# Four-layer graph network on one core: a group's last weighing placed in one TensorE block with the next group's first scores, and new plan constants

## The chip, the cores and the metric

The kernel runs on one core of one Trainium2 chip. The time is the device time of one execution in microseconds (us), the median of three runs. The engines are named as in the profile: PE is TensorE (matrix multiply), PEld its weight load, DVE is VectorE, ACT is ScalarE, POOL is GpSimd, SP is SyncE, which issues the transfers. PSUM is the memory into which PE writes, and which DVE and ACT read.

## The reference, cut to what matters

128 graphs of 64 nodes with 256 features pass four layers, each with its own layer norm, ReLU and residual. Everything is float32.

```python
def reference(x, adj, nodemask, ...):          # x (128, 64, 256), adj (128, 64, 64)
    h = relu(layernorm(x))
    # layer 0: attention, 8 heads of 32, with a mask
    q, k, v = (split_heads(h @ W + b) for W, b in ...)
    scores = einsum('bhqd,bhkd->bhqk', q, k) / sqrt(32)
    attn = softmax(where(adj > 0, scores, NEG))
    x = x + (attn @ v, heads merged) @ Wo + bo
    # layer 1: the same with log(adj + 1e-6) added to the scores
    # layer 2: five steps of a gated graph network
    h = relu(layernorm(x))
    for l in range(5):
        m = h @ weight[l]
        agg = einsum('bij,bid->bjd', adj != 0, m)
        h = gru_cell(agg, h, w_ih, w_hh, b_ih, b_hh)
    x = x + h * nodemask
    # layer 3: a gated graph convolution with three 256 x 256 products
    ...
    return x
```

"Scores" are the products q k, "weighing" is the product of the softmax with v.

## The kernel before

The 128 graphs are worked in 16 groups of 8 graphs (512 tokens). Each group has a front (layers 0 and 1), a chain of five gated steps (layer 2) and a back (layer 3). The kernel doesn't run these in program order: every operation is first recorded in a plan, with a key (where it stands in the pipeline, in units of one group's time), an estimated duration, and what it reads and writes. `Plan.run` then deals the operations out, engine by engine, so that the front of one group, the steps of another and the back of a third stand interleaved in each engine's instruction stream. The order is fixed when the program is built.

```python
INTO, OUT, BESIDE, ALONE = 110, 260, 0.3, 0.1    # ns for going into and out of small matmuls, and weights of choice
AHEAD = 1.5                                       # how far ahead of the oldest operation one may be taken
FRONT, FRONT_LAST, FRONT_SPAN = -0.1, -0.05, 1.0
BACK, BACK_LAST, BACK_SPAN = -0.1, 0.6, 0.5
STEP, STEP_LAST, STEP_SPAN = -0.2, -0.05, 0.4
LOCK, BACK_END, ENTRY = 0.35, 0.05, -0.15
FIRST, FIRST_SPAN = -1.0, 1.05
ORDER = (0, 0, 1, 0, 1, 0)                        # (assignments gathered in one place here)
...
    def bank(name):                               # PSUM: four banks for everything but the gates
        return new("a", [P, 512], 4, name)

    def gate(name):                               # and four for the gates of layer 2
        return new("g", [P, TOK], 4, name)
```

Most matmuls use the whole array (128 rows, 128 columns). Three kinds are small: the scores (64 x 64), the weighing (64 x 32) and the neighbour sum of layer 2, `agg` (64 x 64). The plan marks them `small=True`. Layer 0 or 1 for half a group is one call of `attend`:

```python
    waiting = []

    def attend(layer, xt, half, bias, bias_at, name):
        hT = normed(xt, half, name, True)         # layer norm, ReLU, transposed (lnT on PE)
        ...                                       # q and k products, evacuated to qT and k_exp
        pss = [bank(f"s_{name}_{i}") for i in range(2)]

        def scores():
            ...
                            nc.tensor.matmul(ps[gp * NODES : (gp + 1) * NODES, 2 * c : 2 * c + 2, i, :],   # L585
                                             qT[s, c, t0 : t0 + NODES], k_exp[s, c, :, t0 : t0 + NODES], ...)

        es = [new("e", [P, 4, 2 * NODES], 3, f"e_{name}_{i}") for i in range(2)]
        if waiting:
            weigh_last, reads, po_last, oT_last, finish_last = waiting.pop()

            def both():
                weigh_last()
                scores()

            pe(1440, both, [*reads, qT, k_exp], [*po_last, *pss], holds=[oT_last, *es], small=True)
            finish_last()
        else:
            pe(870, scores, [qT, k_exp], pss, holds=es, small=True)
        ...                                       # v product; softmax on DVE, ACT, POOL; aT: softmax transposed on PE
        po = [bank(f"o_{name}_{i}") for i in range(2)]

        def weigh():
            ...
                            nc.tensor.matmul(o[q * HD : (q + 1) * HD, c, s],                              # L659
                                             v[rows, gp, h * HD : (h + 1) * HD],
                                             aTs[q // 2][rows, 2 * c + q % 2, s], ...)

        def finish():
            ...                                   # oT: evacuated by DVE; y = oT Wo (L672); x = y + x (L675)

        waiting.append((weigh, [v, *aTs], po, oT, finish))

    def flush():
        weigh, reads, po, oT, finish = waiting.pop()
        pe(470, weigh, reads, po, holds=[oT], small=True)
        finish()
```

So the weighing of one half is kept back in `waiting` and placed in one block with the scores of the next half. `both` takes the banks of both, four in all. A group's four halves (two layers, two halves) are driven by `front`, which also loads x for the next group:

```python
    def front(g):
        ...
        for layer in range(2):
            ...
            for half in range(2):
                ...
                attend(layer, xt, half, bias, bias_at, f"{g}_{layer}_{half}")
                yield
        flush()
        if g + 1 < n_groups and g:
            load_x(g + 1)
        ...                                       # A, degrees, adjT (transposed adjacency) for layers 2 and 3
```

and the fronts are recorded one after another:

```python
    parts = {g: front(g) for g in range(n_groups)}
    with plan.strand(FIRST, FIRST_SPAN):
        for g in ORDER:                           # all of group 0, two halves of group 1
            next(parts[g])
        for _ in parts[0]:
            pass
    ...
    begin = {g: g - (LOCK if g + 1 == n_groups else 0.0) for g in range(n_groups)}
    events = sorted([(begin[g] + 0.4 * l, g, l) for g in range(n_groups) for l in range(LAYERS)] +
                    [(begin[g] - 1.001, g, -1) for g in range(1, n_groups)])
    for at, g, l in events:
        last = g + 1 == n_groups
        if l < 0:
            with plan.strand(begin[g] - 1 + FRONT + (FRONT_LAST if last else 0), FRONT_SPAN):
                for _ in parts[g]:
                    pass
            continue
        ...                                       # the entry to layer 2, its five steps, and the back
```

The back uses the four banks too. Its products for half a group, seven in place of eight, accumulate in two of them; DVE adds a saved part and writes F (L1059):

```python
        def total(bk, t, o, i):
            vec(dve(384), lambda: nc.vector.tensor_tensor(
                F[i][:, :, o * P : (o + 1) * P], part(bk), t[:, :3, :], op=ALU.add), [bk, t], [(F[i], o)])
        ...
        product(3, pc)                            # l3c on PE (L1047)
        total(pc, u, 0, 1)
```

Of the kernel before, what the change touches and what calls it, by code (L numbers as in the profile page):

```python
# [44 lines left out]


INTO, OUT, BESIDE, ALONE = 110, 260, 0.3, 0.1
AHEAD = 1.5

FRONT = -0.1
FRONT_LAST = -0.05
FRONT_SPAN = 1.0
BACK = -0.1
BACK_LAST = 0.6
BACK_SPAN = 0.5
STEP = -0.2
STEP_LAST = -0.05
STEP_SPAN = 0.4  # L60
LOCK = 0.35
BACK_END = 0.05
ENTRY = -0.15
FIRST = -1.0
FIRST_SPAN = 1.05
ORDER = (0, 0, 1, 0, 1, 0)
FUSE = -1.05
FUSE_SPAN = 0.45
# [53 lines left out]
class Plan:  # L122
# [62 lines left out]
    def run(self):  # L185
# [12 lines left out]
        for _ in range(len(self.ops)):  # L198
            while due[0] in done:
                due.pop(0)  # L200
            best, horizon = None, due[0].key + AHEAD
            for eng, ops in ready.items():
# [52 lines left out]
def gnn_stack_kernel(ctx: ExitStack, tc: tile.TileContext, a: dict, out: bass.AP):  # L255
# [3 lines left out]
    n_groups = n_pairs // PAIRS  # L259
# [14 lines left out]
    def new(tag, shape, n, name=None):  # L274
        if tag not in tags:
            home = psum if tag in ("a", "g") else dram if tag == "gates" else work
            tags[tag] = Slots(home, tag, n, tag in ("g", "ht", "agg", "Ta", "Th", "gv", "qT", "kexp", "v"))
        return Val(tags[tag], name or tag, shape)

    def bank(name):  # L280
        return new("a", [P, 512], 4, name)
# [4 lines left out]
    def pe(cost, fn, reads, writes, early=0.0, holds=(), small=False):  # L286
        plan.add("PE", cost, fn, reads, writes, early=early, holds=holds, small=small)
# [4 lines left out]
    def vec2(cost, fn, reads, writes, early=0.0):  # L292

        plan.add("DVE", cost, fn, reads, writes, early=early, port=True)
# [4 lines left out]
    def pool(cost, fn, reads, writes, early=0.0):  # L299
        plan.add("POOL", cost, fn, reads, writes, early=early, port=True)  # L300

    def dma(kb, fn, reads, writes, n=1):
        plan.add("SP", max(450 * n, 60 + kb * 5), fn, reads, writes)
# [6 lines left out]
    def load_adj(i):  # L310
        t = new("adjq", [P, n_adj, NODES], 2, f"adjq{i}")
        dma(256, lambda: nc.sync.dma_start(t.tile, adj_t[:, i * n_adj : (i + 1) * n_adj, :]), [], [t])
        adj_vals[i] = [t, None]
# [7 lines left out]
    def load_x(g):  # L321
        t = new("x", [P, PAIRS, D], X_BUFS, f"x{g}")
        x_vals[g] = t
        for half in range(2):
            p = slice(2 * half, 2 * half + 2)
            dma(256, lambda p=p: nc.sync.dma_start(
                t[:, p, :], x_t[:, g * PAIRS + p.start : g * PAIRS + p.stop, :]),
                [], [(t, p.start), (t, p.start + 1)])
# [201 lines left out]
    waiting = []  # L530

    def attend(layer, xt, half, bias, bias_at, name):
# [25 lines left out]
        v = new("v", [P, 2, D], 2, f"v_{name}")  # L558
# [18 lines left out]
        def scores():  # L577
            for i in range(2):
                for c in range(2):
                    for gp in range(2):  # L580
                        for rh in range(2):
                            s = slice(rh * 2 * HD, (rh + 1) * 2 * HD)
                            t0 = (2 * gp + i) * NODES
                            ps = pss[rh].tile.rearrange("p (h i k) -> p h i k", h=4, i=2)
                            nc.tensor.matmul(ps[gp * NODES : (gp + 1) * NODES, 2 * c : 2 * c + 2, i, :],  # L585
                                             qT[s, c, t0 : t0 + NODES], k_exp[s, c, :, t0 : t0 + NODES],
                                             start=True, stop=True)

        es = [new("e", [P, 4, 2 * NODES], 3, f"e_{name}_{i}") for i in range(2)]
        if waiting:  # L590
            weigh_last, reads, po_last, oT_last, finish_last = waiting.pop()

            def both():
                weigh_last()
# [6 lines that stand above are left out]
# [14 lines left out]
        aTs = []  # L615
# [33 lines left out]
        po = [bank(f"o_{name}_{i}") for i in range(2)]  # L649
# [13 lines left out]
        oT = new("oT", [P, 2, 2, P], 1, f"oT_{name}")  # L663
# [12 lines left out]
                xt[:, pp : pp + 2, :], py.tile.rearrange("p (t d) -> p t d", t=2), xt[:, pp : pp + 2, :],  # L676
                op=ALU.add), [py, (xt, pp), (xt, pp + 1)], [(xt, pp), (xt, pp + 1)])

        waiting.append((weigh, [v, *aTs], po, oT, finish))

    def flush():
        weigh, reads, po, oT, finish = waiting.pop()
        pe(470, weigh, reads, po, holds=[oT], small=True)
        finish()

# [261 lines left out]
    def front(g):  # L947

        if g % ADJ_GROUPS == 0 and (g // ADJ_GROUPS + 1) * ADJ_GROUPS < n_groups:
            load_adj(g // ADJ_GROUPS + 1)  # L950
        xt = x_vals.pop(g)
        adjq = adj_vals[g // ADJ_GROUPS][0]
        sel = slice((g % ADJ_GROUPS) * PAIRS, (g % ADJ_GROUPS + 1) * PAIRS)
        first = (g % ADJ_GROUPS) * PAIRS
        neg = new("neg", [P, PAIRS, NODES], 1, f"neg_{g}")
        vec2(200, lambda: nc.vector.tensor_scalar(
            neg.tile, adjq[:, sel, :], 0.0, NEG, op0=ALU.is_le, op1=ALU.mult), [adjq], [neg])
        for layer in range(2):
            if layer and not g % ADJ_GROUPS:
                log_adj(g // ADJ_GROUPS)  # L960
            ladj = adj_vals[g // ADJ_GROUPS][1]
            for half in range(2):
                bias = ladj if layer else neg
                bias_at = (lambda p, t=ladj, n=first: t.tile.rearrange("p t k -> p (t k)")[:, (n + p) * NODES : (n + p + 2) * NODES]) if layer else (
                    lambda p, t=neg: t.tile.rearrange("p t k -> p (t k)")[:, p * NODES : (p + 2) * NODES])
                attend(layer, xt, half, bias, bias_at, f"{g}_{layer}_{half}")
                yield
        flush()
        if g + 1 < n_groups and g:
            load_x(g + 1)  # L970
        for gp in range(2):
            s = slice(gp * NODES, (gp + 1) * NODES)
            pool(530, lambda s=s: nc.gpsimd.tensor_copy(blk[s, :, s], adjq[s, sel, :]), [adjq], [(blk, gp)])

        A = new("A", [P, PAIRS, NODES], 3, f"A_{g}")
        vec2(250, lambda: nc.vector.tensor_scalar(A.tile, adjq[:, sel, :], 0.0, None, op0=ALU.not_equal),
             [adjq], [A])
        deg = new("deg", [P, PAIRS], 2, f"deg_{g}")
        vec(310, lambda: nc.vector.tensor_reduce(
            deg.tile, adjq[:, sel, :], axis=AX.X, op=ALU.add, apply_absolute_value=True), [adjq], [deg])  # L980
        norm = new("norm", [P, PAIRS], 5, f"norm_{g}")
        power(norm, deg, lambda: deg.tile, 1e-6, PAIRS, f"deg_{g}")
        adjT = new("adjT", [P, PAIRS, P], 4, f"adjT_{g}")
        ps = bank(f"adjT_{g}")

        def turn():
            for p in range(PAIRS):
                nc.tensor.transpose(ps[:, p * P : (p + 1) * P], blk[:, p, :], ident.tile)

        pe(437, turn, [blk, ident], [ps], holds=[adjT])  # L990

        for p in range(PAIRS):
            sca(act(P, 1), lambda p=p: nc.scalar.activation(
                adjT[:, p, :], ps[:, p * P : (p + 1) * P], AF.Identity, scale=norm[:, p : p + 1]),
                [ps, norm], [(adjT, p)])
        held[g] = xt, A, adjT, norm
# [138 lines left out]
    parts = {g: front(g) for g in range(n_groups)}  # L1135
    with plan.strand(FIRST, FIRST_SPAN):
        for g in ORDER:
# [8 lines left out]
    with plan.strand(0.5, 0.1):  # L1146
        combine(w3, lambda b: w3[:, :, b, :], 7, made)

    begin = {g: g - (LOCK if g + 1 == n_groups else 0.0) for g in range(n_groups)}
    events = sorted([(begin[g] + 0.4 * l, g, l) for g in range(n_groups) for l in range(LAYERS)] +  # L1150
                    [(begin[g] - 1.001, g, -1) for g in range(1, n_groups)])
    for at, g, l in events:
        last = g + 1 == n_groups
        if l < 0:
            with plan.strand(begin[g] - 1 + FRONT + (FRONT_LAST if last else 0), FRONT_SPAN):
                for _ in parts[g]:
                    pass
            continue
        if l == 0:
            xt, A, adjT, norm = held[g]  # L1160
            with plan.strand(begin[g] + ENTRY, 0.1):
                h, ht = entry(g, xt)
            held[g] = xt, h, adjT, norm
            chains[g] = gru(h, ht, A, str(g))
        with plan.strand(at + STEP + (STEP_LAST if last else 0), STEP_SPAN):
            next(chains[g])
        if l + 1 == LAYERS:
            with plan.strand(begin[g] + 2 + BACK + (BACK_LAST if g + 2 == n_groups else BACK_END if last else 0), BACK_SPAN):
                back(g, *held.pop(g))
# [34 lines left out]
```

## Time and profile before

| | |
|---|---|
| median of 3 runs | 2578.69 us (2578.02 to 2578.84) |
| span of the profiled execution | 2576.9 us |
| PE busy | 2540.9 us |
| PEld busy | 2135.8 us |
| DVE busy | 1866.1 us |
| ACT busy | 1315.1 us |
| POOL busy | 837.8 us |
| mean granted TensorE clock | 0.996 |
| HBM traffic over the span | 55 GB/s |

Busy time is the time in which an engine has at least one instruction in work. Matmuls are pipelined, and each record lasts longer than its share of the stream, so what a matmul costs is read from start to start in the timeline, not from its length. Each matmul of the program leaves two records in the trace. In the timeline a row is a run of like instructions: its start, its length, engine, line, operation, what is written and read, the shapes, the number of records, and in brackets the idle time before it and what ended that.

### The profile page before, as it was taken

Reading aid. Unit: us, or ns where it says so; the run is one execution under the profiler, and the core shown is the slowest. Engines: PE = TensorE matmul, PEld = TensorE weight load, DVE = VectorE, ACT = ScalarE, POOL = GpSimd, SP = SyncE. Lnnn points to the kernel's source line nnn. Section 1 sums busy time; section 2 is a strip of 40 time slices with the busy share of each in tenths; the row PEclk is TensorE's granted clock in tenths of the full one; section 3 lists DMA queues with packets and bytes.
Section 4 is the critical chain, followed back from the end, with each engine's and each line's share of the span. In section 5 each row is a group of like instructions: output and inputs, shape, how many; then the busy total and the mean of one; then the engine's idle time right before and its main releaser. Section 6 shows DMA issues by size and latency. Waiting matters only on the chain.

```text
span 2576.9 us, 54509 instructions
## 1 busy us (share of the span) xinstructions
PE 2540.9 (99%) x22445; PEld 2135.8 (83%) x22445; DVE 1866.1 (72%) x4137; ACT 1315.1 (51%) x2452; POOL 837.8 (33%) x890
## 2 busy tenths in 40 slices
PE   8999999999999999999999999999999999999997
PEld 6788888888888888888888888888888888888885
DVE  5676678777776876778677776777768767776766
ACT  4455454554545546555554545545455455555543
POOL 5442333323232332432323333332323323223220
PEclk9999999999999999999999999999999999999998
DMA  5221211111111111112111111111111111111110
GB/s 155 104 78 44 70 48 57 44 48 60 48 56 44 61 48 48 56 44 68 63 47 57 48 56 48 48 56 48 56 44 60 44 48 56 44 48 70 55 62 17
DMA packets 44203, 145.54 MB, mean 56 GB/s; under 512 B 11106, under 2 KB 32820, under 8 KB 33076
## 3 DMA queue, kind: packets, MB, share of 16 engines
q1 hardware_dynamic: 43840, 142.03, 15.7%
q8 instruction: 177, 2.90, 0.5%
q14 instruction: 70, 0.57, 0.1%
q10 hardware_dynamic: 116, 0.04, 0.0%
HBM read 126.79 MB, written 15.27 MB: 55 GB/s over the span
## 4 chain that ended last, share of the span: by engine, by line
PE 95%; DVE 2%; ACT 2%; issue 0%; DMA 0%; POOL 0%; SPq 0%; DVEq 0%; ACTq 0%; POOLq 0%
PE gb L782 21%; PE gc L782 16%; PE nb L782 10%; PE nc L782 8%; PE q L544 4%; PE k L544 4%; PE y L672 4%; PE v L605 4%; PE agg L822 3%; PE l3b L1047 3%; PE s L585 3%; PE hT L488 2%; PE l3c L1047 2%; PE aT L640 2%; PE lnT L488 2%; PE o L659 2%
## 5 line engine op out<-in xcount | busy, mean ns | idle before, releaser
L891 POOL TENSOR_TENSOR sn<-h,sn 128x512 f32<-128x512 f32 x160 | 205.7, 1286 | 666.8 <-ACT sn L889 666.5
L634 POOL TENSOR_TENSOR e<-e,ssum 128x512 f32<-128x512 f32 x128 | 142.9, 1127 | 344.4 <-DVE ssum L633 279.5
L782 PE MATMUL gb<-Th,w_hh 128*128 128x256 f32 x960 | 247.5, 380 | 1.4 <-DVE sg L854 1.4
L782 PE MATMUL gb<-Ta,gv 128*128 128x256 f32 x960 | 248.0, 381 | 0.0
L751 POOL TENSOR_TENSOR Th<-h 128x256 f32<-128x256 f32 x160 | 122.3, 784 | 351.3 <-PE nb L782 287.2
L889 ACT ACTIVATE sn<-sn,b_n 128x512 f32<-128x512 f32 x160 | 116.2, 726 | 172.6 <-DVE sn L887 155.6
L782 PEld LDWEIGHTS gb<-Th,w_hh 128*128 128x128 f32 x960 | 177.3, 190 | 29.9 <-issue 1.3
L782 PEld LDWEIGHTS gb<-Ta,gv 128*128 128x128 f32 x960 | 176.2, 190 | 23.9 <-issue 2.2
L893 DVE SCALAR_TENSOR_TENSOR sn<-sg,sn 128x512 f32<-128x512 f32 x160 | 112.1, 701 | 109.4 <-POOL sn L891 109.4
L782 PE MATMUL gc<-h,w_hh 128*128 128x256 f32 x640 | 167.4, 384 | 0.5 <-ACT sg L881 0.5
L782 PE MATMUL gc<-agg,gv 128*128 128x256 f32 x640 | 164.3, 379 | 0.0
L874 ACT ACTIVATE sg<-sg,b_rz 128x512 f32<-128x512 f32 x160 | 108.1, 717 | 104.4 <-DVE sg L854 104.3
L782 PE MATMUL nb<-Th,w_hh 128*128 128x256 f32 x480 | 144.4, 383 | 0.0
L782 PE MATMUL nb<-Ta,gv 128*128 128x256 f32 x480 | 143.1, 380 | 0.0
L605 PE MATMUL v<-w_L_gnn_Wv,hT 128*128 128x256 f32 x512 | 141.0, 381 | 0.0
L474 POOL TENSOR_TENSOR rstd<-pw,few 128x2 f32<-128x2 f32 x128 | 104.1, 831 | 106.5 <-DVE pw L473 99.5
L854 DVE TENSOR_TENSOR sg<-gc,ug 128x512 f32<-128x512 f32 x80 | 55.1, 689 | 110.6 <-PE gc L782 109.5
L782 PEld LDWEIGHTS gc<-agg,gv 128*128 128x128 f32 x640 | 121.1, 190 | 16.4
L544 PE MATMUL q<-hT,w_L_gnn_Wq 128*128 128x256 f32 x512 | 133.8, 387 | 0.9 <-ACT hT L493 0.9
L544 PE MATMUL k<-hT,w_L_gnn_Wk 128*128 128x256 f32 x512 | 133.1, 383 | 0.0
L782 PEld LDWEIGHTS gc<-h,w_hh 128*128 128x128 f32 x640 | 116.9, 190 | 18.1 <-issue 2.2
L514 DVE TENSOR_SCALAR xn<-x,mv,rstd 128x256 f32<-128x256 f32 x256 | 112.6, 469 | 26.6 <-ACT ht L518 17.8
(165 smaller groups left out, 6388.4 us busy)
## 6 DMA issues: line engine op xcount, KB each, us to landing
gv<-gates SPq DMA_DIRECT2D x80, 1344.0 KB, 5.9
x<-in_x_dram SPq DMA_DIRECT2D x32, 256.0 KB, 3.0
out_dram<-x SPq DMA_DIRECT2D x32, 256.0 KB, 2.1
gates<-gv SPq DMA_DIRECT2D x5, 1344.0 KB, 5.1
adjq<-in_adj_dram SPq DMA_DIRECT2D x8, 256.0 KB, 2.9
gw<-in_L_gnn_weight_dram SPq DMA_DIRECT2D x5, 256.0 KB, 5.5
w_ih<-in_L_gnn_w_ih_dram SPq DMA_DIRECT2D x2, 384.0 KB, 5.3
w_hh<-in_L_gnn_w_hh_dram SPq DMA_DIRECT2D x2, 384.0 KB
```

The source lines that it names most:

```text
L474: pool(680 if n == 2 else 1220, lambda: nc.gpsimd.tensor_tensor(dst.tile, s.tile, few[:, 1 : 1 + n], op=ALU.pow), [s, (few, 1)], [dst])
L514: vec2(325, lambda p=p, i=i: nc.vector.tensor_scalar(xn[:, i, :], xt[:, p, :], mv[:, i, 0:1], rstd[:, i : i + 1], op0=ALU.subtract, op1=AL ...
L544: pe(mm(256), lambda c=c, kc=kc: nc.tensor.matmul(ps[:, c * HALF : (c + 1) * HALF], wt[:, kc, c * P : (c + 1) * P], hT[:, kc, :], start=kc ...
L605: pe(mm(256), lambda gp=gp, kc=kc: nc.tensor.matmul(pv[:, gp * D : (gp + 1) * D], hT[:, kc, gp * P : (gp + 1) * P], w["v"][:, kc, :], star ...
L634: pool(1000, lambda e8=e8, z=z: nc.gpsimd.tensor_tensor(e8(), e8(), z[:, :, None].to_broadcast(shape), op=ALU.mult), [e, z], [e])
L751: pool(690, lambda: nc.gpsimd.tensor_tensor(T[:, i, :], x(), y(), op=ALU.subtract), reads, [(T, i)])
L782: nc.tensor.matmul(bank_[:, col * HALF : (col + 1) * HALF], at(g, n), rhs(), start=first and j == 0, stop=True, skip_group_check=True)
L874: sca(act(TOK, 1.5), lambda k=k, col=col: nc.scalar.activation(g_v[:, :, k, :], g_v[:, :, k, :], AF.Tanh, bias=b_rz[:, col : col + 1], sca ...
L889: sca(act(TOK, 1.5), lambda: nc.scalar.activation(a_(), a_(), AF.Tanh, bias=b_n[:, oc : oc + 1]), [n_v, b_n], [n_v])
L891: pool(1230, lambda: nc.gpsimd.tensor_tensor(b_(), hh(), a_(), op=ALU.subtract), [*hp, n_v], [n_v])
L893: vec2(dve(TOK, 1), lambda: nc.vector.scalar_tensor_tensor(b_(), z(), 1.0, b_(), op0=ALU.add, op1=ALU.mult), [*ts[1], n_v], [n_v])
L1047: pe(mm(384), lambda: nc.tensor.matmul(bk[:, : 3 * P], b(), w3[:, :, n, :], start=first, stop=True, skip_group_check=True), [w3, *reads], ...
```

## The change

The last weighing of a group is no longer placed by itself. The front of a group now also records the first half of the next group's front, before it ends: `attend` for the next group finds the last weighing of this group in `waiting` and puts it into one block with its own scores. `flush` is left for the case in which nothing has followed (each entry of `waiting` now carries its group's x, so that a flush takes only its own). The load of the next group's x is recorded earlier, since the next group's first half now stands within this front. Eleven constants of the plan are set anew. The description of the change also speaks of keys laid out in passes over all partitions and of durations from the trace; the diff holds no line for either, and the estimated durations of the operations are the same in both kernels.

```diff
-AHEAD = 1.5
-FRONT = -0.1
-FRONT_LAST = -0.05
-FRONT_SPAN = 1.0
+AHEAD = 1.7
+FRONT = 0.1
+FRONT_LAST = 0.1
+FRONT_SPAN = 1.1
 BACK = -0.1
 BACK_LAST = 0.6
-BACK_SPAN = 0.5
+BACK_SPAN = 0.6
 STEP = -0.2
-STEP_LAST = -0.05
+STEP_LAST = -0.1
 STEP_SPAN = 0.4
-LOCK = 0.35
-BACK_END = 0.05
-ENTRY = -0.15
+LOCK = 0.3
+BACK_END = -0.05
+ENTRY = 0.05
 FIRST = -1.0
-FIRST_SPAN = 1.05
+FIRST_SPAN = 1.1
... (attend)
-            weigh_last, reads, po_last, oT_last, finish_last = waiting.pop()
+            _, weigh_last, reads, po_last, oT_last, finish_last = waiting.pop()
...
-        waiting.append((weigh, [v, *aTs], po, oT, finish))
-
-    def flush():
-        weigh, reads, po, oT, finish = waiting.pop()
+        waiting.append((xt, weigh, [v, *aTs], po, oT, finish))
+
+    def flush(xt):
+
+        if not waiting or waiting[-1][0] is not xt:
+            return
+        _, weigh, reads, po, oT, finish = waiting.pop()
         pe(470, weigh, reads, po, holds=[oT], small=True)
         finish()
... (front)
                 attend(layer, xt, half, bias, bias_at, f"{g}_{layer}_{half}")
+                if g and g + 1 < n_groups and layer and not half:
+                    load_x(g + 1)
                 yield
-        flush()
-        if g + 1 < n_groups and g:
-            load_x(g + 1)
+        flush(xt)
... (recording)
+    taken = {g: ORDER.count(1) if g == 1 else 0 for g in range(n_groups)}
...
             with plan.strand(begin[g] - 1 + FRONT + (FRONT_LAST if last else 0), FRONT_SPAN):
+                for _ in range(4 - taken[g]):
+                    next(parts[g])
+                if not last:
+                    next(parts[g + 1])
+                    taken[g + 1] = 1
                 for _ in parts[g]:
                     pass
```

## The prediction

> **What bounds the kernel now.** I read the page's first, second and fourth parts, then PE's waits by stretch, then PE's timeline around the blocks that the change touches. First the page: the busy times, the slices, and the chain that ended last.
>
> ```profile
> span 2576.9 us, 54509 instructions
> ...
> PE 2540.9 (99%) x22445; PEld 2135.8 (83%) x22445; DVE 1866.1 (72%) x4137; ACT 1315.1 (51%) x2452; POOL 837.8 (33%) x890
> ...
> PE   8999999999999999999999999999999999999997
> ...
> PE 95%; DVE 2%; ACT 2%; issue 0%; DMA 0%; POOL 0%; SPq 0%; DVEq 0%; ACTq 0%; POOLq 0%
> ```
>
> PE is busy in every slice, and it is 95% of the chain. Only 2576.9 - 2540.9 = 36.0 us of the span are without a matmul in work. So all that counts is PE's stream: how many matmuls, what each costs from start to start, and where the stream halts. All other engines have slack; POOL's long idle rows cost nothing. Where the 36 us lie, PE's waits over the whole span say (engine, line, what ended the wait, us in total, times, longest):
>
> ```profile
> PE pc L423 <- DMA w_L_gnn_Wv<-in_L_gnn_Wv_dram: 8.8, 1, 8.8
> PE l3b L1047 <- DVE hTT L1036: 4.6, 1, 4.6
> PE lnT L488 <- DVE xn L514: 3.5, 3, 1.8
> PE s L585 <- DVE F L1059: 2.6, 5, 0.5
> ```
>
> The 8.8 us are the first loads, the 4.6 and most of the 3.5 lie in the last 77 us, where one group is left and nothing can be put between its steps. The last matmul starts at 2569.0 us, so some 7.5 us of the end have none. In the long middle, from 240 to 2300 us, PE is busy 2056.2 of 2060 us. Its largest wait there is the fourth line: five times the scores wait for DVE to write F. That is what the change can reach in the middle, with the cost of the block changes, which show as no wait at all. They show in the timeline. First a weighing alone, then a weighing and scores in one block, then scores alone, all from PE's timeline (start, length, line, what, records):
>
> ```profile
> 644.04 0.59 PE L544 MATMUL q<-hT,w_L_gnn_Wq 128*128 128x256 f32 x2
> 644.57 0.86 PE L659 MATMUL o<-aT,v 64*32 64x64 f32 x64
> 645.36 1.13 PE L544 MATMUL q<-hT,w_L_gnn_Wq 128*128 128x256 f32 x4
> 646.32 1.89 PE L672 MATMUL y<-w_L_gnn_Wo,oT 128*128 128x256 f32 x8
> ```
>
> ```profile
> 404.99 1.03 PE L782 MATMUL gb<-Ta,gv 128*128 128x256 f32 x4
> 405.94 0.86 PE L659 MATMUL o<-aT,v 64*32 64x64 f32 x64
> 406.73 1.10 PE L585 MATMUL s<-kexp,qT 64*64 64x128 f32 x32
> 407.76 1.13 PE L782 MATMUL gc<-h,w_hh 128*128 128x256 f32 x4
> 408.73 1.89 PE L672 MATMUL y<-w_L_gnn_Wo,oT 128*128 128x256 f32 x8
> ```
>
> ```profile
> 674.78 0.59 PE L605 MATMUL v<-w_L_gnn_Wv,hT 128*128 128x256 f32 x2
> 675.31 0.43 PE L585 MATMUL s<-kexp,qT 64*64 64x128 f32 x2
> 676.26 1.10 PE L585 MATMUL s<-kexp,qT 64*64 64x128 f32 x30 [0.52 <-DVE F L1059]
> 677.29 0.70 PE L605 MATMUL v<-w_L_gnn_Wv,hT 128*128 128x256 f32 x2
> 677.82 0.81 PE L1047 MATMUL l3b<-w,hTT 128*128 128x384 f32 x2
> ```
>
> Undisturbed, two 256-column records take 0.43 us to the next row and four take 0.86 (y, eight, takes 1.73). Ahead of a small block two take 644.57 - 644.04 = 0.53 and four take 405.94 - 404.99 = 0.95: about 0.095 more. After it four take 646.32 - 645.36 = 0.96 and 408.73 - 407.76 = 0.97: about 0.105 more. The 64 weighing records take 0.79 us in both, whether scores or a full matmul follow. So a small block costs 0.095 + 0.105 = 0.20 us to enter and leave, besides its own matmuls, and going from weighing to scores costs nothing extra. In the third fence the scores start, halt after two records and go on at 676.26: from the first score to the v that follows takes 1.98 us, against 407.76 - 406.73 = 1.03 undisturbed, so the halt costs 0.95 us. Adding up in the same way, over all records of the middle, what each start to start exceeds its typical one gives 8.4 us: 4.7 at these five halts, the rest in pieces of under 0.5 us.
>
> **What the Trainium skill says.** "TensorEngine Tiling (Array Packing)", Key Properties: changing the tiling mode drains TensorE. The trace agrees in kind: 0.20 us for each small block. "Trainium Kernel Development and Optimization", Performance Expectations: matmul busy time is a bad measure, because matmuls are pipelined; hence start to start above. "PSUM — Partial Sum Buffer", Specifications: eight banks of 2 KiB in a partition. The kernel's four banks and four gates are all of them, so scores that want two banks wait for whoever holds them, as the wait for F shows. "TensorE: Matmul & The Clock Gate", Part 1: after some 3.4 us without work the array falls to half clock. The trace shows it at the end alone: after the wait of 4.6 us two 384-column records took 1.42 us (2543.55 to 2544.97) against 0.65 before, and the clock of the last 77 us was 0.88. In the middle it was 1.00, so there is no clock to win there.
>
> **The change part by part.** The changed program, built, can be counted, though not timed.
>
> 1. *Matmuls.* Both programs have the same 12,097 matmuls of the same shapes. Nothing is removed or added there: 0 us.
>
> 2. *Small blocks.* Runs of small matmuls between full ones: before, 48 of weighing with scores, 15 of weighing alone, 14 of scores alone, 77 of agg alone, 3 mixed (two agg with scores, one agg with weighing): 157. After: 63 of weighing with scores, 1 and 1 alone, 80 agg: 145. So 15 pairs are joined and three chance joins with agg are lost: net 12 fewer. 12 x 0.20 = 2.4 us, all on PE's stream, so all of it on the path.
>
> 3. *The waits of lone scores.* The five waits for F are at scores alone, the first half of every other group. In the changed program scores never stand alone after the start. The wait is for a bank, though, not for being alone: l3c's matmul stood 2.2 us ahead of the scores and DVE read it late. In the new order, in a middle group, the first scores of a group stand two rows ahead of that back's first hx, with no l3 product of the group within several us. So I take the five for gone: 5 x 0.95 = 4.7 us.
>
> 4. *New waits.* A joined block needs four banks, the softmax of the one and q and k of the other at once. The 48 joined blocks of before show the price: their mean from first record to the next full matmul is 0.02 us above their typical one, 48 x 0.02 = 1 us in all. For 15 more of them that is 0.3 us. The other constants move fronts later against steps (FRONT and ENTRY by 0.2 of a group) and reorder every engine's stream. I put 1.0 us of new waits in all in the middle, an estimate.
>
> 5. *Start.* Before 240 us PE is idle 60 - 49.94 + 60 - 58.17 + 60 - 57.99 = 13.9 us, of it 8.8 the loads. The first twenty or so rows on each engine are the same. After that the waits seen before (0.9 us at wT, 0.9 at y, 0.9 at gb) meet another order. Some go, some come: -0.5 us.
>
> 6. *End.* The last rows of the programs are the same on every engine: 131 of DVE, 56 of ACT, 44 of POOL, and PE's last 50 or so us. The last 77 us hold most of the idle time that is left, and it stays: 0 us.
>
> 7. *The earlier load of x.* A load takes 3.0 us to land and stands tens of us ahead of its use in both orders: 0 us.
>
> Sum: -2.4 - 4.7 + 1.0 - 0.5 = -6.6 us; from 2578.7 that is 2572.1. As my guess for item 3 is that of waits which may come back elsewhere, I give a little back and say 2573.0 us, 0.22% less.
>
> **Rivals.** *A wait takes the place of those removed.* Where the plan's estimated durations are off, an evacuation comes late at another row, and PE halts again. For it: the plan takes its order from estimates, and 8 us of small halts are in the middle now. Against it: those are 8 us in 2060, by the same planner. It would give 2576 to 2579: the 2.4 us of item 2 less what comes back. *The four banks bind.* Joined blocks hold up both a late softmax and an early set of scores, and PE stands still at each of 15. Against it: the 0.02 us above. At 0.5 us each it would be 2578.7 - 2.4 - 4.7 + 7.5 = 2579. *The fill or the end gets longer.* Group 1's front starts later and the steps of group 0 begin after more of the other work (the first matmul of the steps is the 566th, before the 494th). If PE lacks work there, some 5 us are lost, with the middle's gain about 2578; if the better order fills the 5 us of startup waits, 2568.
>
> **Range and chances.** All that could be won by order is 8.4 us in the middle, 5 at the start and 2.4 from blocks: 2563 is the floor, and 2568 a good outcome. Losses are limited by how evenly this planner fills PE; 5 us of new waits over the estimate make 2578. So 2567 to 2580. Two per cent would be 52 us, more than all of PE's idle time, so faster by that is close to impossible; slower by that would need 3.5 us of halts in each of 15 groups. Chances: 0.01 faster, 0.98 within, 0.01 slower.
>
> **What would show it.** PE busy falls by about 2 to 3 us and the span by 5 to 7; PE's waits for F at L585 are gone; the timeline at a group's last weighing shows o x64, s x32 with 0.79 and 1.03 us; the idle of the last 77 us stays near 17. I am wrong if the middle (240 to 2300) shows PE idle over 6 us, or if the start or the end differ by more than 3 us from before.

## The result, and the profile after

| | before | after |
|---|---|---|
| median of 4 runs each, side by side | 2578.36 us (2576.27 to 2578.84) | 2568.68 us (2568.51 to 2570.03) |
| ratio after to before, 95% interval | | 0.9965 [0.9948, 0.9982] |
| span of the profiled execution | 2576.9 us | 2566.7 us |
| PE busy from 240 to 2300 us | 2056.16 of 2060 us | 2059.75 of 2060 us |
| PE busy in the last 77 us | 59.57 us, clock 0.88 | 58.77 us, clock 0.92 |

The lines of code after `flush` have moved down by three, so L782 is now L785, L1047 is L1050, L1059 is L1062. First the same four lines of the page, of the changed kernel:

```profile
span 2566.7 us, 54470 instructions
...
PE 2534.6 (99%) x22445; PEld 2129.0 (83%) x22445; DVE 1947.9 (76%) x4137; ACT 1308.8 (51%) x2452; POOL 870.4 (34%) x890
...
PE   8999999999999999999999999999999999999997
...
PE 96%; DVE 3%; ACT 0%; DMA 0%; issue 0%; POOL 0%; SPq 0%; DVEq 0%; POOLq 0%
```

The span is 10.2 us shorter, of which 6.3 are PE's busy time and 3.9 its idle time (36.0 to 32.1). DVE works 82 us longer in the sum, and it costs nothing here. PE's largest waits over the whole span of the changed kernel (what waited, what ended the wait, us in total, times, longest):

```profile
PE pc L423 <- DMA w_L_gnn_Wv<-in_L_gnn_Wv_dram: 8.5, 1, 8.5
PE l3b L1050 <- DVE hTT L1039: 5.0, 2, 4.6
PE lnT L488 <- DVE xn L514: 3.6, 3, 2.0
```

The first loads and the two waits of the end are there as before. The fourth line of before, scores waiting for F five times, has no counterpart. From 240 to 2300 us this is the only wait that the trace gives PE:

```profile
PE hT L488 <- ACT h L493: 0.3, 1, 0.3
```

In the timeline of the changed kernel (start, length, line, what, records) a group's last weighing runs into the next group's first scores:

```profile
643.38 0.86 PE L659 MATMUL o<-aT,v 64*32 64x64 f32 x64
644.16 1.10 PE L585 MATMUL s<-kexp,qT 64*64 64x128 f32 x32
645.20 1.13 PE L785 MATMUL gb<-Th,w_hh 128*128 128x256 f32 x4
```

From start to start that is 0.78 and 1.04 us, as in the mixed block of before. In both traces I added up where each start to start exceeds the typical one of its kind, and counted the blocks of small matmuls (157 before, 145 after). So the 10.2 us fall into parts, each good to some 0.4 us, as they depend on what is taken for typical:

| part of the span | predicted | in the traces |
|---|---|---|
| 12 fewer blocks of small matmuls | -2.4 | -2.4 |
| the five halts for F | -4.7 | -4.7 |
| other halts from 240 to 2300 us | +1.0 | -0.4 (3.7 to 3.3) |
| start: the first matmul 0.2 earlier, halts up to 240 us 0.3 less | -0.5 | -0.5 |
| end, from 2300 us on | 0 | -2.2 |
| sum | -6.6 | -10.2 |

The 2.2 us of the end are for the most part a matter of the clock and not won by the change (see the point on the end further on). Without them the change gains 8.0 us in these two traces.

### The profile page after: what moved, and what is told of

The parts are those of the page before. It is cut to its first block, busy times and chain, and to the rows that moved or that the text cites. A ratio compares the mean times of both kernels' runs of the same rounds, so it can differ in the third digit from the quotient of the medians.

```text
span 2566.7 us, 54470 instructions
## 1 busy us (share of the span) xinstructions
PE 2534.6 (99%) x22445; PEld 2129.0 (83%) x22445; DVE 1947.9 (76%) x4137; ACT 1308.8 (51%) x2452; POOL 870.4 (34%) x890
## 4 chain that ended last, share of the span: by engine, by line
PE 96%; DVE 3%; ACT 0%; DMA 0%; issue 0%; POOL 0%; SPq 0%; DVEq 0%; POOLq 0%
PE gb L785 22%; PE gc L785 16%; PE nb L785 11%; PE nc L785 8%; PE q L544 4%; PE v L605 4%; PE k L544 4%; PE y L672 4%; PE agg L825 3%; PE l3b L1050 3%; PE s L585 3%; PE aT L640 2%; PE l3c L1050 2%; PE hT L488 2%; PE lnT L488 2%; PE o L659 2%
## 5 line engine op out<-in xcount | busy, mean ns | idle before, releaser
L894 POOL TENSOR_TENSOR sn<-h,sn 128x512 f32<-128x512 f32 x160 | 211.3, 1321 | 652.1 <-ACT sn L892 652.1
L785 PE MATMUL gb<-Ta,gv 128*128 128x256 f32 x960 | 249.2, 382 | 0.0
L785 PE MATMUL gb<-Th,w_hh 128*128 128x256 f32 x960 | 248.2, 381 | 0.0
L474 POOL TENSOR_TENSOR rstd<-pw,few 128x2 f32<-128x2 f32 x128 | 119.6, 937 | 313.7 <-DVE pw L473 307.3
L785 PEld LDWEIGHTS gb<-Th,w_hh 128*128 128x128 f32 x960 | 179.7, 190 | 27.5 <-issue 2.7
L785 PEld LDWEIGHTS gb<-Ta,gv 128*128 128x128 f32 x960 | 177.0, 190 | 28.7 <-issue 4.1
L785 PE MATMUL gc<-h,w_hh 128*128 128x256 f32 x640 | 166.9, 383 | 0.6 <-ACT sg L884 0.5
L888 DVE SCALAR_TENSOR_TENSOR sn<-sg,sn 128x512 f32<-128x512 f32 x160 | 120.2, 751 | 58.5 <-ACT sn L942 55.6
L785 PE MATMUL gc<-agg,gv 128*128 128x256 f32 x640 | 164.3, 379 | 0.0
L630 ACT ACTIVATE e<-e 128x512 f32<-128x512 f32 x128 | 80.0, 629 | 163.2 <-DVE e L628 161.9
L838 DVE TENSOR_TENSOR Ta<-agg 128x256 f32<-128x256 f32 x160 | 82.8, 557 | 99.0 <-ACT sg L884 36.2
L544 PE MATMUL q<-hT,w_L_gnn_Wq 128*128 128x256 f32 x512 | 148.8, 386 | 1.5 <-DVE e L621 0.8
L544 PE MATMUL k<-hT,w_L_gnn_Wk 128*128 128x256 f32 x512 | 148.9, 382 | 0.0
L785 PE MATMUL nb<-Th,w_hh 128*128 128x256 f32 x480 | 144.4, 382 | 0.0
L785 PE MATMUL nb<-Ta,gv 128*128 128x256 f32 x480 | 143.0, 379 | 0.0
L785 PEld LDWEIGHTS gc<-agg,gv 128*128 128x128 f32 x640 | 121.4, 190 | 19.4
L896 DVE SCALAR_TENSOR_TENSOR sn<-sg,sn 128x512 f32<-128x512 f32 x160 | 112.5, 703 | 31.8 <-POOL sn L894 31.6
L785 PEld LDWEIGHTS gc<-h,w_hh 128*128 128x128 f32 x640 | 118.8, 190 | 19.6 <-issue 2.4
```

Source lines behind the costliest of these rows:

```text
L474: pool(680 if n == 2 else 1220, lambda: nc.gpsimd.tensor_tensor(dst.tile, s.tile, few[:, 1 : 1 + n], op=ALU.pow), [s, (few, 1)], [dst])
L544: pe(mm(256), lambda c=c, kc=kc: nc.tensor.matmul(ps[:, c * HALF : (c + 1) * HALF], wt[:, kc, c * P : (c + 1) * P], hT[:, kc, :], start=kc ...
L785: nc.tensor.matmul(bank_[:, col * HALF : (col + 1) * HALF], at(g, n), rhs(), start=first and j == 0, stop=True, skip_group_check=True)
L888: vec2(dve(TOK), lambda: nc.vector.scalar_tensor_tensor(a_(), r(), 1.0, a_(), op0=ALU.add, op1=ALU.mult), [*ts[0], n_v], [n_v])
L894: pool(1230, lambda: nc.gpsimd.tensor_tensor(b_(), hh(), a_(), op=ALU.subtract), [*hp, n_v], [n_v])
L896: vec2(dve(TOK, 1), lambda: nc.vector.scalar_tensor_tensor(b_(), z(), 1.0, b_(), op0=ALU.add, op1=ALU.mult), [*ts[1], n_v], [n_v])
```

## The experiments

My theory was that of the prediction: the gain is the block changes saved and the halts for F that went, both from the joining, and the constants are there to fit. The rivals: the constants bring the gain and the joining little; a later front alone brings it; the order near the end brings it. There are ten constants, by the lines of the diff, and not eleven as the description above says.

**What a block change costs.** `split_joined` is the changed kernel with a transpose over the whole array between weighing and scores of all 63 mixed blocks. `ahead_of_joined` is its control: the same transpose ahead of the weighing, where the block begins anyway. Both leave a useless result in a bank that the scores then overwrite. (A transpose leaves one record in the trace, not two like the other matmuls.)

```diff
             def both():
                 weigh_last()
+                nc.tensor.transpose(pss[0][:, :P], ident.tile, ident.tile)    # split_joined
                 scores()
```

> The changed kernel with one full-array transpose, whose result is overwritten, between the weighing and the scores of each of the 63 joined blocks: the order of everything else is the same, and 62 more small blocks are entered and left (207 in place of 145). If a block costs 0.20 us: 63 x (0.20 + 0.11 for the transpose itself) = 19.5 us more than the changed kernel, 2588 us. If entering and leaving is hidden behind other work: the transposes alone, 63 x 0.11 = 6.9 us more, 2575.6 us.

> Control for the run before: the same 63 transposes at the head of the joined blocks, where they part nothing (145 blocks). Both theories: 63 x 0.11 = 6.9 us more than the changed kernel, 2575.6 us. The difference of the two runs, divided by 63, is the cost of entering and leaving a block.

`split_joined` took 2585.38 us (2585.11 to 2586.18), ratio 1.0028 [1.0017, 1.004]; `ahead_of_joined` 2577.02 us (2575.92 to 2578.09), 0.9999 [0.999, 1.0007]. A block of `split_joined` in PE's timeline, in the same columns:

```profile
635.28 0.86 PE L660 MATMUL o<-aT,v 64*32 64x64 f32 x64
636.07 0.33 PE L595 MATMUL s<-ident 128*128 128x128 f32 x1
636.32 1.10 PE L585 MATMUL s<-kexp,qT 64*64 64x128 f32 x32
637.36 1.13 PE L786 MATMUL gb<-Ta,gv 128*128 128x256 f32 x4
```

From weighing to the matmul after the scores: 637.36 - 635.28 = 2.08 us, against 645.20 - 643.38 = 1.82. The 0.26 are 0.11 for the transpose itself and 0.15 for leaving small matmuls and entering them again. 63 x 0.26 = 16.4, and the kernel took 16.7 us more than the changed one. The control took 8.3 more, where its transposes account for 6.9. The difference of the two is 8.36 / 63 = 0.13 us for each split. That the timeline says 0.15 fits what the end shows: the control's last 75.25 us, from the last row of eight hx records on, are the same matmuls that take 73.93 in `split_joined`, and (8.36 + 1.32) / 63 = 0.15. So a block change is a real cost on PE's stream. The prediction's 0.20 was for a matmul of 256 columns behind the block (0.105 of it); the transpose behind the block pays 0.055 in its place, which makes 0.095 + 0.055 = 0.15.

**Joining and constants apart.** The change has two halves, and each was run without the other: the changed code with the ten old constants, and the code of before with the ten new ones.

```diff
 joined_old_constants: the changed kernel, with
-AHEAD = 1.7
-FRONT = 0.1
-FRONT_LAST = 0.1
-FRONT_SPAN = 1.1
+AHEAD = 1.5
+FRONT = -0.1
+FRONT_LAST = -0.05
+FRONT_SPAN = 1.0
 ... and the other six as before
 apart_new_constants: the kernel before, with the same ten lines the other way round
```

> The changed kernel with the constants of the plan as they were before; the joining and the earlier load of x stay. The built program has 146 small blocks (157 before, 145 after). If the joining is the cause: 11 x 0.20 = 2.2 us from the blocks and the five halts of lone scores at F (4.7 us) gone, less about 1 us of new halts, so about 2572.5 us. If the constants are the cause: only the 2.2 us of the blocks, about 2576 us, with halts in the middle of 4 us or more, as before.

> The kernel before with the new constants alone: nothing joined across groups. The built program has 158 small blocks. If the joining is the cause: no gain from blocks, lone scores stand in the middle again and may halt for F or another bank's reader, 2576 to 2580 us. If the constants are the cause: about 2571 us, the result less the 2.4 us of the blocks.

| | old constants | new constants |
|---|---|---|
| weighing apart from the next group's scores | 2578.36 us | 2806.00 us, ratio 1.0887 [1.0871, 1.0903] |
| joined | 2597.43 us, ratio 1.0077 [1.0062, 1.0092] | 2568.68 us, ratio 0.9965 [0.9948, 0.9982] |

Both expectations failed, mine and the rivals'. Against the kernel before, which took 2577.56 us beside these two, the joining alone costs 20 us though it has 146 blocks and no scores that wait for F; the constants alone cost 228; together they gain 10. The reasons are in the waits. In `joined_old_constants` the halts of the middle add up to 26.2 us, against 8.4 before and 3.3 after; the largest are gates waiting for `sg`, DVE's sum for them. In `apart_new_constants` PE stands at a product of the back that waits for `hTT`, the differences that DVE makes for the seven products. First the wait of `joined_old_constants` (from 240 to 2300 us), then that of `apart_new_constants` (whole span):

```profile
PE gb L785 <- DVE sg L857: 6.4, 11, 0.6
PE l3b L1047 <- DVE hTT L1036: 98.8, 14, 8.0
```

PE's and DVE's timeline of `apart_new_constants` around one of its halts shows why:

```profile
1035.01 0.81 PE L1047 MATMUL l3c<-w,hT 128*128 128x384 f32 x2
...
1040.86 1.26 DVE L1126 SCALAR_TENSOR_TENSOR x<-o,x 128x256 f32<-128x256 f32 x1
...
1043.44 0.28 DVE L1036 TENSOR_TENSOR hTT<-hT,hTT 128x128 f32<-128x128 f32 x1
...
1043.86 1.62 PE L1047 MATMUL l3b<-w,hTT 128*128 128x384 f32 x2 [8.04 <-DVE hTT L1036]
```

DVE isn't idle here: it works through a softmax and layer norm of a front (L626 to L633, L508 to L514) and the closing sums of the half before in the back (L1126), all of which stand ahead of the 0.28 us of `hTT` in its fixed order. Front and back have fallen on one stretch, in which PE has no gated step to fill in with. The halt costs more than its 8.04 us: behind it the two records take 1.42 us to the next row (1043.86 to 1045.28) where they take 0.64 before it (1034.37 to 1035.01), half clock. Added up from start to start, what PE loses at half clock is, by my estimate, some 30 of the 228 us.

**Which of the constants.** Five kernels set only a part of them anew.

```diff
 joined_late_fronts:   joined; only FRONT, FRONT_LAST and ENTRY new
 joined_early_fronts:  joined; all new but these three
 apart_early_fronts:   apart;  all new but these three
 joined_old_ahead:     joined; all new but AHEAD
 joined_fronts_first:  joined; FRONT, FRONT_LAST, ENTRY, FRONT_SPAN and FIRST_SPAN new
```

> The joined kernel with three of the new constants, those that set fronts and entries 0.15 to 0.2 of a group later (FRONT, FRONT_LAST, ENTRY); all others as before. Theory: the joining records a quarter of each front one group earlier, and these three put the fronts back to where they stood, so they alone make the joining pay: about 2571 us (2568.7 to 2576). Rival: the new constants work only as a whole set: near joined_old_constants, 2590 us or more.

> The joined kernel with all new constants but FRONT, FRONT_LAST and ENTRY, which stay as before. Theory of the late fronts: near joined_old_constants, 2590 to 2600 us. Rival (another constant of the set, such as AHEAD, carries it): 2575 us or less.

> Not joined, with all new constants but FRONT, FRONT_LAST and ENTRY. Theory of the late fronts: the 227 us that the new constants cost without joining come from the late fronts falling together with the backs, so without them the time is near that of before, 2574 to 2590 us, with no waits of 8 us at l3b. Rival (AHEAD or the longer spans are to blame): 2700 us or more. The built program has 160 small blocks, 3 more than before: 0.6 us of it.

> The changed kernel with AHEAD back at 1.5, all other constants new. If AHEAD (how far ahead of the oldest operation one may be taken) is what the joined order needs: 2585 us or more. If it is one constant among equals: 2569 to 2575 us.

> The joined kernel with the new constants of the fronts and of the start (FRONT, FRONT_LAST, FRONT_SPAN, ENTRY, FIRST_SPAN), but AHEAD, BACK_SPAN, BACK_END, STEP_LAST and LOCK as before. If the joined front, which holds more, needs the longer span as well as the later place: 2569 to 2574 us. If only the whole set works: 2585 us or more.

| | median, us | ratio to before, 95% interval | halts in the middle, us |
|---|---|---|---|
| joined_late_fronts | 2591.45 | 1.0055 [1.004, 1.007] | 10.6 |
| joined_early_fronts (three executions; a stray one of 10 ms left out) | 2592.20 | 1.0059 [1.0043, 1.0076] | 23.8 |
| apart_early_fronts | 2587.67 | 1.0043 [1.0028, 1.0058] | 19.6 |
| joined_old_ahead | 2762.68 | 1.0721 [1.0699, 1.0742] | some 183, half clock included |
| joined_fronts_first | 2759.86 | 1.071 [1.0689, 1.0731] | some 180, half clock included |

None of these parts of the set pays. `joined_late_fronts` has a middle nearly as good as that of before, but its start halts for 33.4 us instead of 19.6, so the theory that later fronts alone make the joining pay falls. Without joining, the later fronts and entries are what costs: 2806.0 with them, 2587.7 with early ones, the other new constants being the same. In the joined kernel, `joined_fronts_first` differs from `joined_late_fronts` by the two spans of 1.1 alone, and is 168 us slower. `joined_old_ahead` has all the rest as well, and is as slow. Its largest wait from 240 to 2300 us:

```profile
PE l3b L1050 <- DVE hTT L1039: 47.8, 12, 4.1
```

It is the same wait at the same place in the back, 12 times about 4 us, and AHEAD = 1.7 takes it away. So in the joined kernel, late and longer fronts need operations to be taken from further ahead. Why 1.5 isn't enough there, by the plan's own choices, I didn't follow further; that stays open. Open too is whether constants fitted to the kernel that isn't joined would gain as much as the change does: no run looked for such constants, so nothing here shows that the gain needs the joining.

**The halts for F without the joining.** In the timeline of DVE of the kernel before, the operation that the scores waited for:

```profile
675.04 0.69 DVE L885 SCALAR_TENSOR_TENSOR sn<-sg,sn 128x512 f32<-128x512 f32 x1 [1.28 <-ACT sg L874]
675.65 0.55 DVE L1059 TENSOR_TENSOR F<-l3c,lu 128x384 f32<-128x384 f32 x1
```

F's sum stood behind L885, and DVE waited 1.28 us for ACT with it in hand. `scores_no_halt` is the kernel before with that one sum (of the third l3c product) given a key 1 us earlier, so that it stands ahead of L885.

```diff
-        total(pc, u, 0, 1)
+        total(pc, u, 0, 1, early=1000.0)     # key moved forward by 1000 ns
```

> The kernel before, with its constants and nothing joined; only the addition of the saved part to the third l3c product (L1059, the DVE instruction for which lone scores wait) gets a key 1 us earlier. In the built program it and its product then stand a few rows earlier, and the rows around them are dealt anew; the small blocks stay at 157. If the five halts cost 0.95 us each and are a matter of that DVE instruction's place: they go and 4.7 us with them, about 2572.5 us. If they are a matter of lone scores as such, or come back elsewhere: 2576 to 2579 us.

It took 2587.04 us (2585.89 to 2588.04), ratio 1.0039 [1.0024, 1.0054]: slower. The five halts are gone, and two waits have come in their place, here from 240 to 2300 us:

```profile
PE hx L1083 <- DVE o L1113: 6.0, 11, 0.5
PE hT L488 <- DVE h L895: 5.6, 11, 0.5
```

Both are waits of transposes (hx and hT, of h). Eleven groups have both, each of which costs 0.65 to 0.7 us from start to start: some 14 us for the 4.7 won. Before each one DVE has a row of three times its usual length, each time L1106 with 1.26 or 1.27 us. From the timeline of `scores_no_halt`, DVE, POOL and PE:

```profile
681.39 1.31 POOL L634 TENSOR_TENSOR e<-e,ssum 128x512 f32<-128x512 f32 x1 [0.94 <-DVE ssum L633]
681.72 1.26 DVE L1106 TENSOR_TENSOR F<-F,r_L_gnn_b_t 128x256 f32<-128x256 f32 x1
...
683.73 0.63 PE L488 MATMUL hT<-ident,h 128*128 128x128 f32 x4 [0.50 <-DVE h L895]
```

L1106 usually takes 0.42 us (its median). Here it starts 0.33 us after a POOL operation and ends 0.28 us after it: 681.39 + 1.31 = 682.70, 681.72 + 1.26 = 682.98. The Trainium skill, "SBUF — State Buffer", Who interferes with whom, says that DVE and GpSimd share one pair of SBUF ports under an exclusive lock, that a DVE instruction with two SBUF inputs contends with a GpSimd instruction that reads SBUF, and that the order of issue decides which of them blocks. The trace agrees, POOL having started first: L1106 is held up by 0.84 us, so h, which DVE writes next (682.91), is late, and PE halts for 0.50. The plan keeps the two apart by its estimates (it has a lock for them), but their real times have moved on one another. No run here takes the POOL operation away, so this reading rests on the trace and the page.

**The end.** `tail_filled` puts 36 useless transposes, 3.9 us, ahead of the place where PE waits 4.6 us for hTT near the end. `tail_plain` takes the wait itself away: one more half group, the first half of the last but one, has the eight plain products instead of seven, so that no hTT is needed there.

```diff
 tail_plain
-        if g + 1 == n_groups:
+        if g + 1 == n_groups or (g + 2 == n_groups and half == 0):
             plain_products(hT, F, f"{g}_{half}")
 tail_filled, in seven_products, for the same half
+            def full():
+                for i in range(36):
+                    nc.tensor.transpose(pf[:, (i % 4) * P : (i % 4 + 1) * P], ident.tile, ident.tile)
```

> The changed kernel, with plain products in place of the seven for one half of the last group but one, so that nothing there waits for the differences hTT on DVE. PE does 0.65 us more of its own. If the wait of 4.6 us for hTT sets the end: it goes, the half clock after it too, and PE then waits for h (ready 6.3 us after the wait began) behind 5.2 us of plain products: 3 to 6 us less than the changed kernel, 2563 to 2566 us. If DVE's chain sets the end anyhow: the same 2568.7 us within 1.

> The changed kernel with 36 full-array transposes of no use (3.9 us) placed where PE waits 4.6 us for hTT near the end; every other instruction stands as in the changed kernel. If the slow matmuls after that wait come from PE's standing still (half clock): the wait shrinks to under 1 us, the l3b and l3c rows after it take 0.65 us in place of 1.3, and 2 to 3 us go: 2566 us. If they are slow for another reason: no change, 2568.7 us.

`tail_plain` took 2564.83 us (2564.45 to 2566.55), ratio to before 0.9955 [0.9938, 0.9972]: the lowest time of all, as the first case had it. The interval overlaps that of the changed kernel, 0.9965 [0.9948, 0.9982], and the two didn't run side by side; the traces show the gain more clearly. From the last row of eight hx records to the end it takes 69.95 us instead of 73.35. The 4.6 us wait is gone; part of it comes back as a longer one at lnT (up to 2.8 us, 2.0 in the changed kernel). `tail_filled` took 2568.07 us (2565.62 to 2568.45), 0.9963 [0.9948, 0.9977], no different from the changed kernel where 2566 was expected, but its clock tells something. The first products behind the wait, in `tail_filled` and then in the changed kernel:

```profile
2533.58 0.88 PE L1050 MATMUL l3b<-w,hTT 128*128 128x384 f32 x2 [1.00 <-DVE hTT L1039]
```

```profile
2533.99 1.31 PE L1050 MATMUL l3b<-w,hTT 128*128 128x384 f32 x2 [4.62 <-DVE hTT L1039]
```

These and the three rows of two products that follow, up to the next hx, take 2.85 us where PE has worked during the wait (2533.58 to 2536.43) and 4.35 where it has stood still (2533.99 to 2538.34): half clock. So the slow products do come from PE's standing still. But the 1.5 us are lost again later: after the waits for lnT and hT in the last group, four gate matmuls of 512 columns take 3.42 us up to the next row in `tail_filled` and 2.29 in the changed kernel, and the four transposes behind them 0.81 and 0.43.

## Why the prediction was right, point by point

I said 2573.0 us, and it is 2568.68, inside the range. The ratio foreseen, 2573.0 / 2578.7 = 0.9978, lies inside the measured interval. The span fell by 10.2 us where I had named 5 to 7; the 2.2 us of the end, luck for the most part, make up most of the difference.

- *Blocks* (12 x 0.20): right. 12 fewer in the trace; the cost of a change was measured by `split_joined` and its control.
- *The five halts for F* (5 x 0.95): right in size, and the scores no longer stand behind a bank that F holds, as I said. But that isn't the work of the joining: in `apart_early_fronts` and `apart_new_constants` 16 blocks of scores stand alone, more than before, and none of them waits for F. Any of the new orders took these halts away, and all but the changed kernel's brought others. What the joining by itself is shown to save are the 2.4 us of the blocks. That PE's busy time fell by 6.3 and not by the 2 to 3 I named is my slip of reckoning: a halt of 0.95 us from start to start shows as 0.52 of idle time, and the rest counts as busy, so 2.1 us of these halts (5 x 0.43) stood in the busy time from the beginning.
- *New waits in the middle* (+1.0): too much. The middle has small delays of some 0.3 us in each of 12 groups, in two places (q after k, aT after y), 3.3 us in all, and the other halts of before, 3.7 us, are gone. The step is off by 1.4 us.
- *Start* (-0.5): right in the sum.
- *End* (0): here the prediction failed by 2.2 us, within the 3 us I had allowed. "The last rows of the programs are the same on every engine" is true, but the same rows don't take the same time. In the kernel before, then in the changed one, the products after the same two waits of 1.41 and 0.69 us:

```profile
2510.62 1.52 PE L1047 MATMUL l3b<-w,hT 128*128 128x384 f32 x2 [0.69 <-ACT hT L493]
2511.93 1.49 PE L1047 MATMUL l3c<-w,hT 128*128 128x384 f32 x2
```

```profile
2502.19 0.91 PE L1050 MATMUL l3b<-w,hT 128*128 128x384 f32 x2 [0.69 <-ACT hT L493]
2502.94 0.81 PE L1050 MATMUL l3c<-w,hT 128*128 128x384 f32 x2
```

From the first row to the second it is 1.31 us before and 0.75 after: half clock there, nearly the 0.65 of full clock here. From the lnT row ahead of it to the next agg row, the same sequence of matmuls, it took 7.1 us in six of the 14 traces and 6.0 in eight. `joined_late_fronts` and `scores_no_halt` are among the slow, `split_joined` and `apart_early_fronts` among the fast, so it goes with neither half of the change; and `ahead_of_joined`, slow, differs from `split_joined` only in where its transposes stand. The clock in the traces says what it goes with. It changes in pieces of 3.41 us, and where these begin differs from trace to trace. In the kernel before, both waits fall into one piece (2507.39 to 2510.80), in which PE worked 1.31 us, and the next piece has half clock. In the changed kernel a boundary falls into the first of the waits (at 2500.18), PE worked 2.17 and 2.27 us in the two pieces, and the clock stays full. So it is in all 14: the piece with least work has at most 1.60 us in the six slow traces and at least 1.88 in the eight fast ones. The prediction had half clock at the wait of 4.6 us alone and overlooked it here.

Behind the wait of 4.6 us it is the same: two pieces at half clock in the kernel before, one in the changed kernel, and the products from there to the next hx row take 5.03 us (2543.55 to 2548.58) and 4.35. Together that is 1.8 of the 2.2 us. As the boundaries of the pieces fall differently on the same rows from trace to trace, I call these 1.8 us luck. Repeated executions differ by more than that: 18 of the kernel before, in one session, took 2575.77 to 2579.24 us.

- *The load of x*: right, PE waits for no x.

Of the rivals, none came about in the changed kernel. But "a wait takes the place of those removed" is what happened in every variant with another order of the middle: the joined kernel with any constants but its own, both variants that aren't joined, and `scores_no_halt`. My case against it, "8 us in 2060, by the same planner", was thin: the same planner with nearly the same program also makes 26 us of halts in the middle, or some 180. What spoke for the changed kernel was rather that its ten constants were set anew together with its structure, and I gave that no weight.

## What to carry to other kernels

Where one engine is 99% busy and the order is fixed at build time, count two things from the trace: what is switched (0.2 us per block of small matmuls here) and where the bottleneck's stream halts, from start to start and not by idle time. A change of structure and the constants of its schedule are one change: each alone cost 20 and 228 us here, together they gained 10. So give neither the credit before both have been run alone, and fit the constants again after each change of structure.

## What the runs showed of the hardware

- *Half clock after short pauses.* The Trainium skill, "TensorE: Matmul & The Clock Gate", Part 1, puts the fall to half clock after at least one idle window of about 3.4 us, in windows that run freely. Here pauses of 1.41 and 0.69 us, with transposes between them, brought half clock in six traces and not in eight, by how they fell on pieces of 3.41 us. That the same pauses hit or miss fits windows that run freely; that 2.1 us of pause are enough, with 1.31 to 1.60 us of work beside them, doesn't fit a window that must be wholly idle. The measurement decides. How much work keeps the clock full isn't fixed by these traces: in `joined_fronts_first` a piece with 1.42 us of work (from 1697.97 us) was followed by full clock.
- *DVE held up by POOL.* DVE's busy time rose from 1866.1 to 1947.9 us with the same 4137 instructions. In both traces each DVE instruction that lasts over 0.06 us longer than the short ones of its kind (their tenth percentile) runs beside one of POOL; what these last longer adds up to 57 us before and 130 after. The plainest case is `neg`, 16 instructions: their median is 280 ns before and 1358 ns after. In DVE's and POOL's timeline of the changed kernel:

```profile
725.96 1.66 POOL L611 TENSOR_TENSOR x<-x,r_L_gnn_bo 128x512 f32<-128x512 f32 x1 [0.55 <-DVE xn L514]
...
726.41 1.36 DVE L959 TENSOR_SCALAR neg<-adjq 128x256 f32<-128x256 f32 x1
```

POOL's operation ends at 727.62 us, DVE's at 727.77: DVE's instruction lasts until POOL's is done, and 0.15 us more. In the kernel before, the neg at 736.26 us started when POOL was idle, and took 0.28 us. Busy time of DVE is thus partly waiting, and a longer one needn't mean more work.
